# Edge stage of a four-layer graph network: TensorE in source order, layer 0's products spread over the batches, edge arrays loaded alone, and a short last batch

## The chip, the cores and the metric

The kernel runs on one core of a Trainium2 chip. The metric is the device time of one execution in microseconds. A core has TensorE (PE, with its weight loads shown apart as PEld), VectorE (DVE), ScalarE (ACT), GpSimd (POOL) and SyncE (SP). SP, ACT and POOL also issue DMA transfers, which 16 DMA engines carry out.

## What is computed

There are 3125 nodes with 128 features each, and 103,125 edges (`src`, `dst`, `edge_weight`) sorted by `dst`. Four layers follow one another, each with a residual and a layer norm:

```python
x = _layernorm(x + _L0_gnn_ref(x, src, dst, edge_weight, ...))  # relu(segment_sum(w * (x @ W)[dst], src) + b)
x = _layernorm(x + _L1_gnn_ref(x, edge_index, ...))             # four attention heads over the edges, skip, norm
x = _layernorm(x + _L2_gnn_ref(x, ...))                         # attention over the edges, one head
x = _layernorm(x + _L3_gnn_ref(x, edge_index, ...))             # two mean aggregations, sigmoid
```

The kernel turns the edges into two dense matrices over (dst, src), padded to 3200 x 3200: `wd` in DRAM, float32, holds the sums of the edge weights, and `f_ctd` in DRAM, bf16, holds the number of edges. Layer 0 multiplies with `wd`; the other layers use `f_ctd`.

## The kernel before, in words

`fast_path` does the work (`general_path` stands in a branch that runs only if a check at the end fails).

**Front.** The three edge arrays are loaded (lines 584 to 586; `dst` and the weights by SP, `src` by ACT), VectorE and ScalarE pack them into `tab` (628 to 630), and SP and ACT store it to the DRAM table `td` (633). POOL then gathers from `td` five groups of 128 windows (648, tile `eg`). A window is five destination rows; it gets 256 consecutive edges. In the program the load of `x` (642, 644) stands ahead of the gathers, and the 25 loads of weights, biases and attention vectors (through `load` at 540, and 713) are on ACT's DMA queue; some of them are issued before the edges' table is stored.

**Keys.** `keys_of(g)` (from line 655) turns group `g` into keys: VectorE and ScalarE make `kic`, `kid` and `wei` (661 to 669), TensorE transposes them in six pieces into PSUM (674 to 676), and copies out of PSUM give `kd2`, `kc2` and the three bf16 parts of the weight (534, 536, 689, 692, 693). Groups 0 and 1 are made in the front, groups 2 to 4 while batches 9, 17 and 25 run (`make(b)`, at `b % 8 == 2`).

**Edge stage.** There are NBT = 40 batches of BW = 16 windows, 640 windows, though 625 hold the 3125 rows. `make(b)` has VectorE write one-hot matrices for the batch's 32 half-windows: `ohd` and `ohc` (826), and `wod`, the first times each part of the weights (835); ScalarE makes a quarter of the last part (844). `make(b + 1)` stands ahead of batch b's products. A batch has four groups of four windows. For a group TensorE runs eight products into `cp` (866) and 24 into `wp` (874); ScalarE copies them out to `cs` (879) and `ws` (885). `cp` and `wp` share three PSUM banks. The tiles `ohd` and `ohc` have two buffers each, `wod` six (two batches), `ws` and `cs` two. After a batch SP stores `ws` to `wd` (887, two transfers, pieces of 512 bytes), and after every second batch `cs` to `f_ctd` (890, pieces of 320 bytes).

**Layer 0's products.** The sum over nodes runs over 25 blocks of 128 rows of `wd`. For the first Z0 = 20 column blocks `add0` (786) loads a block's rows in two tiles `cw` (792, 640 KB each; three buffers) and runs 20 products, 40 TensorE instructions, in one go (796). The loop calls it for a block once its rows are stored: `while acc0 and (done + 1) * P <= (b - 1) * BW * WN`. Blocks that are left after the loop follow it. The remaining five column blocks are added after the stage, in tiles `left` (PSUM) out of 320 KB loads. `xw_of` (747) makes `xw = x @ W` in batches 0 and 1, and `products_of_weights` (728 to 743) small products in batch 2.

**Order.** Each engine's order of instructions is set by a scheduler from the program; none of it is fixed by hand. DMA transfers of one queue are issued in that queue's order, and an issue can wait for an earlier transfer to land.

After the edge stage come layer 1 (from about 545 us of the profile), layer 2 and layer 3. The change doesn't touch them.

Of the kernel before, what the change touches and what calls it, by code (L numbers as in the profile page):

```python
# [7 lines left out]
F32 = mybir.dt.float32  # L8
# [486 lines left out]
NBT = NW // BW  # L495
Z0 = 20
# [11 lines left out]
def fast_path(  # L508
# [29 lines left out]
    def load(name, ap, shape):  # L538
        t = cst.tile(shape, F32, name=name)
        nc.scalar.dma_start(t, ap)  # L540
        return t
# [100 lines left out]
    nc.sync.dma_start(x[:, 0:NF, :], x_in[0 : NF * P, :].rearrange("(b p) d -> p b d", p=P))  # L642
    nc.gpsimd.memset(x[:, NF, :], 0.0)
    nc.sync.dma_start(x[0:NR, NF, :], x_in[NF * P : N, :])
    egs = []
    for g in range(NG):
        eg = ep.tile([P, EW // 16, 3, 16], F32, name="eg", bufs=3)
        nc.gpsimd.indirect_dma_start(
# [3 lines left out]
        egs.append(eg)  # L652

    def keys_of(g):

        eg = egs[g]
        kd2 = kp.tile([P, P // BW, 2, BW, 2], BF16, name="kd2")
        kc2 = kp.tile([P, P // BW, 2, BW, 2], BF16, name="kc2")
        w2 = [kp.tile([P, P // BW, 2, BW, 2], BF16, name=f"w2_{s}") for s in range(3)]
# [10 lines left out]
        t0 = cps.tile([P, 4, P], F32, name="t0", tag="cw")  # L670
        t1 = cps.tile([P, 2, P], F32, name="t1", tag="cw")
        for h in range(2):
            a = slice(h * P, (h + 1) * P)
            nc.tensor.transpose(t0[:, h, :], kid[:, a], ident)
            nc.tensor.transpose(t0[:, 2 + h, :], kic[:, a], ident)
            nc.tensor.transpose(t1[:, h, :], wei[:, a], ident)
# [9 lines left out]
        for h in range(2):  # L686
            copy(kd2[:, :, h, :, :], pairs(t0, h))
            copy(kc2[:, :, h, :, :], pairs(t0[:, 2:, :], h))
            nc.scalar.copy(w2[0][:, :, h, :, :], pairs(t1, h))
        for s, (i, o) in enumerate(((t1, wt), (wt, wu))):  # L690
            for h in range(2):
                nc.vector.tensor_tensor(each(o, h), each(i, h), w2[s][:, :, h, :, 0], OP.subtract)
                nc.scalar.copy(w2[s + 1][:, :, h, :, :], pairs(o, h))
        return kd2, kc2, w2, wu

    keys = {0: keys_of(0), 1: keys_of(1)}


    l0_wt = load("f_l0_wt", l0_w, [P, P])
# [11 lines left out]
    for s, a in enumerate((l1_as, l1_ad)):  # L711
        for h in range(H):
            nc.scalar.dma_start(att[h * C : (h + 1) * C, s * H + h : s * H + h + 1], a[h, :].rearrange("(c o) -> c o", o=1))
# [72 lines left out]
    def add0(pool, i, accs, blocks):  # L786

        b0, n = blocks
        for h in range(0, n, 10):
# [5 lines left out]
            for j in range(h, h + m):  # L795
                nc.tensor.matmul(  # L796
                    accs[j // 4][:, j % 4, :], cw[:, j - h, :], xw[:, i, :], start=False,
                    stop=(i == NB - 1 and (j % 4 == 3 or j == n - 1)), skip_group_check=True,
                )
# [12 lines left out]

    def make(b):

        if b % 8 == 2 and 8 < b < NBT - 8:
            keys[b // 8 + 1] = keys_of(b // 8 + 1)
# [7 lines left out]

        for o, k in ((ohd, kd2), (ohc, kc2)):
            nc.vector.tensor_tensor(  # L826
                o.rearrange("p w (a t) -> p w a t", t=2), twos(k),
                ramp.rearrange("p (a t) -> p a t", t=2)[:, None, :, :].to_broadcast([P, 2 * BW, P // 2, 2]),
                OP.is_equal,
            )  # L830
        wod = []
        for s in range(3):
            f = of_.tile([P, 2 * BW, P], BF16, name="wod")
            n = 2 * BW if s < 2 else BW
            nc.vector.tensor_tensor(  # L835
                f[:, 0:n].rearrange("p w (a t) -> p w a t", t=2), ohd[:, 0:n].rearrange("p w (a t) -> p w a t", t=2),
                twos(w2[s])[:, 0:n], OP.mult,
            )
            wod.append(f)

# [9 lines left out]
    done = 0  # L850
    cur = make(0)
    for k in range(0, BW, 4):
        cur[3](k)
    for b in range(NBT):
        ohd, ohc, wod, _ = cur
        cur = make(b + 1) if b + 1 < NBT else None
        if b % SB == 0:
# [768 lines left out]
```

## Time and profile before

| what | us |
|---|---|
| median of three runs | 1529.78 (1528.83 to 1531.31) |
| profiled execution | 1529.55 |
| its span, first to last instruction | 1527.5 |
| PE, DVE, ACT, POOL busy in the span | 1395.1, 978.3, 921.5, 127.8 |
| first gather of edges issued (POOL) | 23.28 |
| first one-hot matrix begun (DVE) | 31.67 |
| last one-hot work of the last batch ends (DVE) | 460.97 |
| last of layer 0's first 20 column blocks ends (PE) | 499.0 |

Times are microseconds from the span's start. A group's line gives the source line, the engine, the operation, the tiles written and read, the shapes, the count, then the busy time and the mean of one in ns, then the idle time of the engine before them with what ended it. A line of waits says which engine and line waited for which, and then the total, the number of waits and the longest. In the timeline each line is a start and a duration. In the table of stages each line is a stretch, its length, the busy time (and instructions) of PE, PEld, DVE, ACT and POOL, then the granted TensorE clock as a share of full speed, the share of the 16 DMA engines' time, and GB/s.

### The profile page before, as it was taken

To read this page: it belongs to the slowest core of one execution; us is meant where nothing else is said; L and a number is where in the kernel's file an instruction comes from. 1 tells how busy PE (TensorE), PEld (TensorE's weight loads), DVE (VectorE), ACT (ScalarE), POOL (GpSimd) and SP (SyncE) were. 2 spreads that over 40 slices of the span, in tenths; PEclk is the share of its full clock that TensorE was granted. 3 is DMA by queue.
4 is the path that set the end of the run, shared out by engine and by line. 5 is a ranking of instruction groups with operands and counts; after the bars stand their busy time and mean duration, and the time that the engine had idled before them with its cause. 6 is when DMAs were issued, how large, how long until landed. Compare 5 with 4: busy or idle time off the path is not lost. (4 is left out here: it accounts for less than half of the span.)

```text
span 1527.5 us, 35222 instructions
## 1 busy us (share of the span) xinstructions
PE 1395.1 (91%) x14871; PEld 1220.8 (80%) x14871; DVE 978.3 (64%) x1574; ACT 921.5 (60%) x1880; POOL 127.8 (8%) x162
## 2 busy tenths in 40 slices
PE   4899999999997987999989989899999989999995
PEld 3898999998997876889979979577777764458995
DVE  4999899999991389879978887444464360012005
ACT  2988778888882479878778677554465330023006
POOL 2000000000000023203212310300000000000000
PEclk9999999999999999999999999999999999999998
DMA  6387787887878633444434433232222227513551
GB/s 193 87 216 212 208 227 206 236 211 208 221 211 246 207 97 97 142 125 122 131 119 117 132 86 104 79 111 70 76 61 78 69 100 250 196 44 130 195 195 46
DMA packets 210370, 223.92 MB, mean 147 GB/s; under 512 B 72893, under 2 KB 184008, under 8 KB 209946
## 3 DMA queue, kind: packets, MB, share of 16 engines
q1 hardware_dynamic: 206344, 217.26, 48.9%
q10 hardware_dynamic: 3457, 2.35, 0.6%
q8 instruction: 118, 1.93, 0.5%
q0 software_dynamic: 400, 1.97, 0.4%
q14 instruction: 51, 0.41, 0.1%
HBM read 157.19 MB, written 64.36 MB: 145 GB/s over the span
## 5 line engine op out<-in xcount | busy, mean ns | idle before, releaser
L1243 PE MATMUL acc<-vp,cm 128*128 128x198 bf16 x2500 | 345.7, 253 | 7.5 <-DVE cm L1228 4.6
L1227 ACT ACTIVATE fm<-adr,bas 128x896 bf16<-128x896 f32 (+1 forms) x320 | 286.3, 952 | 67.6 <-DVE cm L1228 62.8
L1238 PE MATMUL acc<-vp,ct 128*128 128x204 bf16 x1250 | 315.3, 256 | 9.0 <-DVE vp L1146 4.5
L1243 PEld LDWEIGHTS <-cm 128*128 128x128 bf16 x2500 | 236.2, 98 | 26.8 <-issue 9.3
L874 PE MATMUL wp<-wod,ohc 128*128 128x128 bf16 x3840 | 244.0, 219 | 8.9 <-ACT cs L879 6.6
L874 PEld LDWEIGHTS <-ohc 128*128 128x128 bf16 x3840 | 224.0, 98 | 10.0 <-issue 9.5
L835 DVE TENSOR_TENSOR wod<-ohd,w 128x4096 bf16<-128x4096 bf16 (+1 forms) x120 | 225.0, 1929 | 0.6 <-PE wp L874 0.6
L1228 DVE TENSOR_TENSOR cm<-fm,ct 128x896 bf16<-128x896 bf16 (+1 forms) x320 | 196.6, 645 | 36.0 <-PE acc L1243 13.6
L844 ACT ACTIVATE wod<-ohd,wu 128x128 bf16<-128x128 bf16 x640 | 197.0, 399 | 0.0
L1382 DVE TENSOR_TENSOR e<-e,ct 128x416 f32<-128x416 f32 (+1 forms) x175 | 108.3, 625 | 106.2 <-ACT e L1381 98.1
L1381 ACT ACTIVATE e<-s,f_nm 128x416 f32<-128x416 f32 (+1 forms) x175 | 109.6, 633 | 97.8 <-PE s L1378 90.8
L1386 PEld LDWEIGHTS acc<-self__8127,e 128*128 128x128 f32 x1250 | 148.2, 193 | 20.6 <-issue 18.8
L1386 PE MATMUL acc<-self__8127,e 128*128 128x129 f32 x1250 | 148.6, 276 | 0.6 <-DVE e L1382 0.6
L1378 PE MATMUL s<-yT,f_xT 128*128 128x416 f32 (+1 forms) x350 | 142.8, 543 | 4.6 <-ACT rt L1358 4.0
L796 PE MATMUL acc<-f_xw,cw 128*128 128x128 f32 x1000 | 119.2, 279 | 7.5 <-DMA cw<-wd 7.5
L1238 PEld LDWEIGHTS <-ct 128*128 128x128 bf16 x1250 | 122.7, 98 | 2.6 <-issue 1.4
L885 ACT COPY ws<-wp 128x512 f32<-128x512 f32 x160 | 93.5, 585 | 49.9 <-PE wp L874 48.3
L796 PEld LDWEIGHTS acc<-f_xw,cw 128*128 128x128 f32 x1000 | 115.8, 195 | 7.8 <-DMA cw<-wd 7.7
L866 PE MATMUL cp<-ohc,ohd 128*128 128x125 bf16 x1280 | 96.7, 218 | 21.1 <-ACT ws L885 17.9
L1378 PEld LDWEIGHTS s<-yT,f_xT 128*128 128x128 f32 x350 | 62.1, 191 | 55.5 <-issue 39.2
L1555 PE MATMUL acc<-ip,ct 128*128 128x128 bf16 x1875 | 105.2, 219 | 0.0
L826 DVE TENSOR_TENSOR ohd<-kd,ramp 128x4096 bf16<-128x4096 bf16 x40 | 91.5, 2288 | 21.2 <-PE cp L866 21.1
(279 smaller groups left out, 1492.9 us busy)
## 6 DMA issues: line engine op xcount, KB each, us to landing
ct<-f_ctd SPq DMA_DIRECT2D x50, 800.0 KB
wd<-ws SPq DMA_DIRECT2D x40, 896.0 KB
ct<-f_ctd SPq DMA_DIRECT2D x150, 224.0 KB
cw<-wd SPq DMA_DIRECT2D x50, 640.0 KB
f_ctd<-cs SPq DMA_DIRECT2D x20, 1000.0 KB
ct<-f_ctd SPq DMA_DIRECT2D x25, 416.0 KB
ct<-f_ctd SPq DMA_DIRECT2D x25, 365.2 KB
cw<-wd SPq DMA_DIRECT2D x25, 320.0 KB
```

Of the source, the lines that this page charges most:

```text
L796: nc.tensor.matmul(accs[j // 4][:, j % 4, :], cw[:, j - h, :], xw[:, i, :], start=False, stop=(i == NB - 1 and (j % 4 == 3 or j == n - 1)) ...
L835: nc.vector.tensor_tensor(f[:, 0:n].rearrange("p w (a t) -> p w a t", t=2), ohd[:, 0:n].rearrange("p w (a t) -> p w a t", t=2), twos(w2[s] ...
L844: nc.scalar.activation(wod[2][:, BW + w, :], ohd[:, BW + w, :], AF.Copy, scale=w3[:, 1, at : at + 1])
L874: nc.tensor.matmul(wp[:, j, :], ohc[:, w, :], wod[s][:, w, :], start=(j == 0 and q == 0 and s == 0), stop=(j == 3 and q == 1 and s == 2), ...
L1227: nc.scalar.activation(f[:, : n * P], at, AF.Relu, bias=bas[:, c, h : h + 1], scale=UP)
L1228: nc.vector.tensor_tensor(m[:, : n * P], f[:, : n * P], ct[:, : n * P], OP.min)
L1238: nc.tensor.matmul(out_(F1, PW), ct[:, k * P : (k + 1) * P], vp[:, c, hp : hp + 2, :, 2 * F1 : V1], start=(c == 0), stop=False, skip_group ...
L1243: nc.tensor.matmul(out_(0, 2 * F1)[:, j], ms[j][:, k * P : (k + 1) * P], vp[:, c, hp + j, :, 0 : 2 * F1], start=False, stop=(c == NB - 1 a ...
L1378: nc.tensor.matmul(s[:, :m], xT[:, c * P : (c + 1) * P], yT[:, i0 * P + a : i0 * P + a + m], start=True, stop=True)
L1381: nc.scalar.activation(e[:, a : a + m], s[:, :m], AF.Exp, bias=nm[:, q : q + 1], scale=scale)
L1382: nc.vector.tensor_tensor(e[:, a : a + m], e[:, a : a + m], ct[:, a : a + m], OP.mult)
L1386: nc.tensor.matmul(acc[k // 3][:, (k % 3) * (P + 1) : (k % 3 + 1) * (P + 1)], es[q, c][:, k * P : (k + 1) * P], vo[:, c, 0 : P + 1], start ...
```

## The change

1. From batch 3 on, TensorE's instructions keep the program's order (`manual_schedule` for PE) until the end of the edge stage. The scheduler still orders the other engines.
2. `adds0` issues a block's loads at once and returns its 20 products as a list. The loop runs them from the next batch on: three after each group, four after the second, 13 a batch.
3. The load of `x` waits (through two POOL memsets of `x`) until the second gather is issued; the weights' loads go to SP's queue behind `x`, with the exception of `l0_wt` and `l0_br`.
4. `keys_of` is split: `columns_of` two batches ahead, at `b % 8 == 1`, and the transposes at `b % 8 == 3`. The transposes go through two PSUM tiles that ScalarE copies to SBUF (`k_` in bf16, `w_`), and the other copies read those. Group 1 is no longer made in the front.
5. The last batch has LW = 4 windows and one group in place of four; VectorE writes 4 windows per half there. 628 windows give 3140 rows; the remaining 60 rows of `wd` are filled with zeros by six stores after batch 6 (10 rows each, in pieces of 25 numbers, 100 bytes). The unused columns of the last `cs` are set to zero by POOL.
6. The last store of `f_ctd` is issued by ACT.

```diff
 def load(name, ap, shape):
     t = cst.tile(shape, F32, name=name)
-    nc.scalar.dma_start(t, ap)
+    with tc.issue_after(x_load.ins):
+        nc.sync.dma_start(t, ap)
     return t
...
-    nc.sync.dma_start(x[:, 0:NF, :], x_in[0 : NF * P, :].rearrange("(b p) d -> p b d", p=P))
-    nc.gpsimd.memset(x[:, NF, :], 0.0)
-    nc.sync.dma_start(x[0:NR, NF, :], x_in[NF * P : N, :])
     egs = []
     for g in range(NG):
...
+        if g == 1:
+            with tc.issue_after(got.ins):
+                nc.gpsimd.memset(x[:, 0:1, 0:1], 0.0)
+                nc.gpsimd.memset(x[:, NF, :], 0.0)
+    x_load = nc.sync.dma_start(x[:, 0:NF, :], x_in[0 : NF * P, :].rearrange("(b p) d -> p b d", p=P))
+    nc.sync.dma_start(x[0:NR, NF, :], x_in[NF * P : N, :])
...
+    def keys_of(kid, kic, wei):
...
+        k_ = ep.tile([P, 4, P], BF16, name="k_")
+        w_ = ep.tile([P, 2, P], F32, name="w_")
+        t = cps.tile([P, 4, P], F32, name="t", tag="cw")
         for h in range(2):
...
+            nc.tensor.transpose(t[:, h, :], kid[:, h * P : (h + 1) * P], ident)
+            nc.tensor.transpose(t[:, 2 + h, :], kic[:, h * P : (h + 1) * P], ident)
+        nc.scalar.copy(k_, t)
+        t = cps.tile([P, 4, P], F32, name="t", tag="cw")
+        for h in range(2):
+            nc.tensor.transpose(t[:, h, :], wei[:, h * P : (h + 1) * P], ident)
+        nc.scalar.copy(w_, t[:, 0:2, :])
...
-    keys = {0: keys_of(0), 1: keys_of(1)}
+    keys = {0: keys_of(*columns_of(0))}
...
-    def add0(pool, i, accs, blocks):
+    def adds0(pool, i, accs, blocks):
...
+        todo = []
...
-                nc.tensor.matmul(
+                todo.append(lambda j=j, a=cw[:, j - h, :]: nc.tensor.matmul(
...
+        return todo
...
-        if b % 8 == 2 and 8 < b < NBT - 8:
-            keys[b // 8 + 1] = keys_of(b // 8 + 1)
+        if b % 8 == 1 and b < NBT - 8:
+            keys[b // 8 + 1] = columns_of(b // 8 + 1, marked)
+        if b % 8 == 3 and b < NBT - 8:
+            keys[b // 8 + 1] = keys_of(*keys[b // 8 + 1])
...
+        def some(s):
+            if b < NBT - 1:
+                return [slice(0, 2 * BW if s < 2 else BW)]
+            return [slice(0, LW)] + ([slice(BW, BW + LW)] if s < 2 else [])
...
+        nw = BW if b < NBT - 1 else LW
+        todo += soon
+        soon.clear()
...
-        for k in range(0, BW, 4):
+        for k in range(0, nw, 4):
...
             nc.scalar.copy(ws[:, k : k + 4, :], wp)
+            m = 4 if k == 4 else 3
+            for f in todo[:m]:
+                f()
+            del todo[:m]
...
+        if b == 6:
+            nc.vector.memset(none, 0.0)
+            for i in range(NL * WN, NP, 10):
+                with tc.issue_after(stored.ins):
+                    nc.sync.dma_start(
+                        wd[i : i + 10, :].rearrange("i (p k) -> p i k", p=P), none.rearrange("p (i k) -> p i k", k=NB)
+                    )
...
+            eng = nc.scalar if b == NBT - 1 else nc.sync
+            eng.dma_start(ctd[:, :, i0 : i0 + SB * BW * WN].rearrange("c d i -> d c i"), cs)
...
+            order = ExitStack()
+            order.enter_context(tc.manual_schedule(engines={mybir.EngineType.PE}))
         while acc0 and (done + 1) * P <= (b - 1) * BW * WN:
-            add0(zp, done, acc0, (0, Z0))
+            soon += adds0(zp, done, acc0, (0, Z0))
             done += 1
+    for f in todo + soon:
+        f()
+    order.close()
     for i in range(done, NB):
         add0(zp, i, acc0, (0, Z0))
```

In the changed kernel's own order of SP's queue the six zero stores stand directly behind the stores of batch 6, and directly ahead of the loads of block 2 (rows 256 to 383).

## The prediction

> **What bounds the kernel now.** I read the page first. PE is busy in 91% of the span, but its chain of waits is mostly in later layers, which the change leaves alone. So I took the edge stage (31 to 499 us) apart: VectorE's groups and waits there, then the timelines of DVE, PE and the front.
>
> VectorE's groups and its longest wait between 30 and 500 us:
>
> ```profile
> L835 DVE TENSOR_TENSOR wod<-ohd,w 128x4096 bf16<-128x4096 bf16 (+1 forms) x120 | 225.0, 1929 | 0.6 <-PE wp L874 0.6
> L826 DVE TENSOR_TENSOR ohd<-kd,ramp 128x4096 bf16<-128x4096 bf16 x40 | 91.5, 2288 | 21.2 <-PE cp L866 21.1
> L826 DVE TENSOR_TENSOR ohc<-kc,ramp 128x4096 bf16<-128x4096 bf16 x40 | 91.4, 2284 | 0.0
> ...
> DVE ohd L826 <- PE cp L866: 21.1, 16, 1.7
> ```
>
> VectorE is the stage's pace: 225 + 91.5 + 91.4 = 408 us of a stretch of 429 (31.67 to 460.97). It stands still only where PE frees `ohd` late, 16 times, 21.7 us with the 0.6 above. The cause is PE's order:
>
> ```profile
> 425.11 0.60 PE L866 MATMUL cp<-ohc,ohd 128*128 128x125 bf16 x8
> 425.55 1.50 PE L874 MATMUL wp<-wod,ohc 128*128 128x128 bf16 x24
> 426.89 0.60 PE L866 MATMUL cp<-ohc,ohd 128*128 128x125 bf16 x8
> ...
> 428.28 4.68 PE L796 MATMUL acc<-f_xw,cw 128*128 128x128 f32 x40
> 432.80 0.55 PE L874 MATMUL wp<-wod,ohc 128*128 128x128 bf16 x7
> ```
>
> A group takes 426.89 - 425.11 = 1.78 us, a batch of four 7.12. A block of layer 0 holds PE for 432.80 - 428.28 = 4.52 us at once, 0.226 per product. A block is due every 128/80 = 1.6 batches, so PE needs 7.12 + 4.52/1.6 = 9.95 us a batch on the mean. VectorE's own batch (ohd 450.97 to the end of wod 460.97, less overlap) is 2.2 + 2.2 + 5.54 = 9.95 too. Both engines are level, and 4.5 us lumps make one wait for the other.
>
> The stage's end, PE's timeline, then two stretches of one microsecond (the clock and the DMA share are the last but two and last but one columns):
>
> ```profile
> 470.90 9.24 PE L796 MATMUL acc<-f_xw,cw 128*128 128x128 f32 x80
> 487.63 11.39 PE L796 MATMUL acc<-f_xw,cw 128*128 128x128 f32 x80 [7.49 <-DMA cw<-wd]
> ```
> ```profile
> 482.00:483.00 1.00, 0.00 (x0) 0.00 (x0) 0.00 (x0) 0.00 (x0) 0.00 (x0) 1.00 1.22 249
> ...
> 488.00:489.00 1.00, 1.00 (x6) 1.00 (x6) 0.00 (x0) 0.00 (x0) 0.00 (x0) 0.50 1.04 430
> ```
>
> Four blocks are left when the edges end; two of them wait 7.5 us for loads that queue behind the last `f_ctd` store, and the idle PE falls to half its clock (0.50) and needs until 492 to recover, some 2.4 us lost. From VectorE's end to the stage's end: 499.0 - 461.0 = 38.0 us.
>
> The front: the timeline has the table's store issued at 13.78 and the gather at 23.28.
>
> ```profile
> 13.78 1.69 SPq L633 DMA_DIRECT2D td<-tab  x1
> ...
> 23.28 1.20 POOL L648 DMA_INDIRECT eg<-td,row_i  x1 [11.86 <-DMA f_att<-in_L_gnn_att_dst_dram]
> ...
> 27.62 0.35 DVE L661 TENSOR_SCALAR kic<-eg,thr 128x256 f32<-128x256 f32 x1 [9.82 <-DMA eg<-td,row_i]
> ```
>
> **The change, part by part** (against the profiled execution: 1529.55, of which 2.05 lie outside the span; the median of the three runs, 1529.78, is the same).
>
> *Front, gain 5.5.* The last piece of `src` is issued at 5.26, behind weights; without them at about 3.7, and it took 2.6 to be read (7.96): about 1.6 earlier. Three casts leave VectorE's way to `tab`: 0.4. So `td` is stored at 11.8. Its 1.25 MB then share the engines with nothing; before, the 1.57 MB of `x` lay ahead. Bounds: 9.5 us as now, or 3.6 (1.25 MB at the 350 GB/s of that stretch) plus 1.5; I take 7.0, so the gather goes at 18.8 and `kic` follows 4.3 later (23.28 to 27.62), with half a us for the `x` beside it at 23.7, 3.9 earlier. From `kic` to the first one-hot is 4.05 now; the new path adds a copy (0.6, as `ws`) but makes `ohc` first: about 3.2. Only one group's keys are made: the last `wod` of batch 0 ends at 26.9 + 2.2 + 0.5 + 2.2 + 0.5 + 5.5 = 37.8, now 43.3. The later `x` (issued near 22, landed near 30) is needed at 31.8 at the earliest. Its 25 followers on SP lie ahead of the first `wd` store, at about 45; if the attention vectors' small loads hold SP as they hold ACT's queue now (6.2 + 2.7 us) they end near 36. Uncovered, that costs up to 5.
>
> *Spreading, gain 21.7.* A group with three products takes 1.78 + 0.68 = 2.46, a batch with 13 products 10.06; no lump is left. Fixed order asks that ACT keep up: two copies at 0.47 apart and four activations at 0.295, 2.1 us a group, under 2.46.
>
> *Keys, about 0, then a cost of 4.5.* VectorE pays 0.6 (kic, kid) plus about 1.5 for four groups (its `kc` copies read SBUF; 0.17 to 0.42 each by the small casts and the present `kc`, 0.25 taken), about as much as now. But ACT now runs six copies ahead of `cs` and waits for VectorE's `wt` and `wu`; `ws` of the second group then comes near 9.7 us after the batch's start while PE wants its bank at 8.3. About 1.5 us for each of three groups; bounds 0 and 4.6 in all by ACT's present waits there (`kd` on `kc`, 4.6).
>
> *Last batch, gain 7 on VectorE.* Nine operations on 4 windows at 0.28 (an eighth of 2.29) to 0.4, 3.0 in all, in place of 9.95. PE: one group, 1.78, in place of 7.12. A zeroing on idle POOL is hidden by 30 batches of slack.
>
> *The tail.* 22 blocks and part of the 23rd are run in the loop by the loop's arithmetic (13 a batch; 27 products are left at the end of batch 38). Batch 38 needs 10.06 after VectorE ends it. Then one group, 27 products (6.1), and blocks 23 and 24 (9.1); loads are bounded by three buffers and the last stores, so I count 20, not 17. ACT's own issue of the last `f_ctd` takes it out of SP's way.
>
> *Zero stores, the one new cost that I think shows: 13.* 60 rows go out as 60 x 128 = 7680 pieces of 100 bytes. They stand behind batch 6's store and ahead of block 2's loads on SP, and PE, in fixed order, reaches block 2 after two groups and seven older products of batch 7, plus a third group: 2.46 + 2.69 + 1.78 = 6.9 us on. The nearest row is `f_ctd`: pieces of 320 bytes moved at 203 to 259 GB/s in 480 to 485, 14.4 GB/s an engine, 22 ns a piece. Then 480 pieces an engine take 10.6 us, from about 3.5 us into the batch (after the 1.02 MB of `wd`), and the 640 KB load lands near 17.5: PE stands for 10.6 and pays 2.4 at half clock. No row has pieces under 320 bytes written in number: at half the price the stall is 5, at double 21 to 26; if PE lags or the loads slip past, 0. I take the row's own 22 ns.
>
> [...]
>
> [...]
>
> *Sum.* VectorE: 37.8, seven batches of 9.95 and two key items (2.1) give 109.5; batch 7 on PE takes 10.06 + 13: 132.6. From there PE is the later engine: 31 batches at 7.12 = 220.7, 387 products at 0.2266 = 87.7, transposes 2.0, plus 4.5 (keys), 3 (three loads issued within 8 us of their need, one every eight batches) and 2 (batches in which VectorE is longer): 452.5. Tail 20: 472.5 against 499.0, so 26.5 less: **1503**. The rest of the kernel should shift as a whole.
>
> **Rivals.**
> - *Zero stores hidden.* VectorE then runs on to 424.3 for batch 38; 10.1 + 3 + 20 give 459, about 40 less: 1489 (1486 to 1496). For: DMA engines are 0.79 to 0.84 busy there, not full. Against: one queue, in order, and a PE that can't pass the load.
> - *Zero stores at double price, or more loads late:* gains of 5 to 19, 1510 to 1526.
> - *Slower: loads late for every block.* PE cannot run another group while a `cw` is missing. The DMA share rises with the faster batch, 0.82 x 10.75/10.1 = 0.87. If each of 22 blocks makes PE wait, each us of it costs 22 us; from 1.4 us a block on, the 29.5 to the slower side is eaten, and at 2 us it would be about 1547. Against: a load now takes some 9 us from issue to use even behind 2 MB of stores, and most are issued 10 us or more ahead.
> - *No effect:* the front and the last batch alone give 5.5 + 7, so this needs a new wait of the same size.
>
> **Chances.** Forecast (1496 to 1510) 0.45; hidden 0.22; dearer but faster 0.20; within 0.2%, about what a measurement of this kernel can tell from no change, 0.03; slower 0.10. Faster 0.87. The range 1485 to 1522 takes in the first two cases and most of the third.
>
> **What would show it.** `kic` near 23.7 and the first full `wod` at 37.8; VectorE's waits for `cp` gone outside batch 7 to 9; one PE wait for `cw` of some 10 us near 116, with a clock of 0.5 after it; the stage ending near 472. Wrong: repeated PE waits for `cw`, or for `ws` in ordinary batches, or a wait of PE at `x` or SP at the weights in the front.

## The result and the profile after

| | before | after |
|---|---|---|
| median of 4 runs each, taken in turn (us) | 1529.43 (1528.83 to 1531.31) | 1542.78 (1540.93 to 1545.23) |
| ratio, 95% interval | | 1.0085 (1.0072 to 1.0098) |
| span of the profiled execution (us) | 1527.5 | 1539.7 |
| mean granted TensorE clock | 0.981 | 0.966 |
| edge stage ends (us) | 499.0 | 511.4 |

The change is slower by 13 us; 1503 was forecast, and even the range's upper end, 1522, is missed. The whole loss lies in the edge stage: it ends 12.4 us later, the span 12.2.

VectorE's groups of the changed kernel from 20 to 545 us, and its longest wait there (sum, times, longest):

```profile
L881 DVE TENSOR_TENSOR wod<-ohd,w 128x4096 bf16<-128x4096 bf16 (+2 forms) x122 | 221.4, 1865 | 0.4 <-PE wp L926 0.4
L870 DVE TENSOR_TENSOR ohd<-kd,ramp 128x4096 bf16<-128x4096 bf16 (+1 forms) x41 | 90.1, 2199 | 46.8 <-PE cp L918 46.8
L870 DVE TENSOR_TENSOR ohc<-kc,ramp 128x4096 bf16<-128x4096 bf16 (+1 forms) x41 | 89.8, 2192 | 0.4 <-PE wp L926 0.2
...
DVE ohd L870 <- PE cp L918: 46.8, 28, 20.0
```

VectorE's work went down by 6.6 us (401.3 for 407.9), nearly the 7 of the last batch. Its wait for PE, which the change was to remove, went up from 21.1 to 46.8 us, and one wait of 20.0 is nearly half of it. PE's timeline in batch 7 of the changed kernel shows what PE did then:

```profile
118.70 1.11 PE L821 MATMUL acc<-f_xw,cw 128*128 128x128 f32 x8
119.65 0.60 PE L918 MATMUL cp<-ohc,ohd 128*128 128x125 bf16 x8
120.09 1.50 PE L926 MATMUL wp<-wod,ohc 128*128 128x128 bf16 x24
141.72 1.65 PE L821 MATMUL acc<-f_xw,cw 128*128 128x128 f32 x6 [20.13 <-DMA cw<-wd]
143.16 1.05 PE L918 MATMUL cp<-ohc,ohd 128*128 128x125 bf16 x8
144.00 1.85 PE L926 MATMUL wp<-wod,ohc 128*128 128x128 bf16 x24
```

PE stands for 20.13 us in front of one product of block 2, whose `cw` isn't there; the groups behind it have all they need. SyncE's queue in the same time (start, time taken by the issues), and the stretches of 5 us (after the engines' busy times: granted clock, DMA share, GB/s):

```profile
106.06 11.74 SPq L943 DMA_DIRECT2D wd<-ws  x4
117.85 12.39 SPq L948 DMA_DIRECT2D wd<-none  x6
130.35 4.57 SPq L817 DMA_DIRECT2D cw<-wd  x3
```
```profile
120.00:125.00 5.00, 1.59 (x29) 1.42 (x26) 4.29 (x6) 4.73 (x15) 0.00 (x0) 0.92 1.21 102
125.00:130.00 5.00, 0.00 (x0) 0.00 (x0) 0.00 (x0) 0.00 (x0) 0.00 (x0) 0.50 1.53 42
130.00:135.00 5.00, 0.00 (x0) 0.00 (x0) 0.00 (x0) 0.00 (x0) 0.00 (x0) 0.50 1.28 38
135.00:140.00 5.00, 0.00 (x0) 0.00 (x0) 0.00 (x0) 0.00 (x0) 0.00 (x0) 0.50 0.95 117
```

The six zero stores (`wd<-none`) stand ahead of the loads, their issue alone takes SyncE 12.39 us, and while they run the transfer engines are full (share over 1) but move only 38 to 42 GB/s. At 40 GB/s over 16 engines a piece of 100 bytes takes 40 ns; the forecast took 22. All four engines stand still, and PE's clock falls to 0.50.

The same shape comes back in small every eighth batch. PE's timeline in batch 15, then stretches of 1 us:

```profile
224.61 1.50 PE L926 MATMUL wp<-wod,ohc 128*128 128x128 bf16 x24
228.90 0.94 PE L821 MATMUL acc<-f_xw,cw 128*128 128x128 f32 x6 [2.79 <-DMA cw<-wd]
229.67 0.70 PE L918 MATMUL cp<-ohc,ohd 128*128 128x125 bf16 x8
230.17 2.77 PE L926 MATMUL wp<-wod,ohc 128*128 128x128 bf16 x24
```
```profile
228.00:229.00 1.00, 0.10 (x1) 0.10 (x1) 0.08 (x2) 0.77 (x3) 0.00 (x0) 1.00 1.01 415
...
230.00:231.00 1.00, 1.00 (x14) 1.00 (x11) 0.52 (x1) 0.58 (x1) 0.00 (x0) 0.52 0.71 292
231.00:232.00 1.00, 1.00 (x13) 1.00 (x11) 1.00 (x1) 0.00 (x0) 0.00 (x0) 0.50 0.15 55
```

A wait of 2.79 us is followed by some 3 us at half the clock, in which 24 matmuls take 2.77 us instead of 1.50. The length of the wait doesn't decide this. A longer one, in batch 23, leaves the clock at 1.00, and a shorter one, in batch 36, halves it (the last section says when):

```profile
317.07 0.94 PE L821 MATMUL acc<-f_xw,cw 128*128 128x128 f32 x6 [3.57 <-DMA cw<-wd]
...
318.28 1.50 PE L926 MATMUL wp<-wod,ohc 128*128 128x128 bf16 x24
...
461.77 0.49 PE L821 MATMUL acc<-f_xw,cw 128*128 128x128 f32 x2 [2.36 <-DMA cw<-wd]
...
462.87 2.77 PE L926 MATMUL wp<-wod,ohc 128*128 128x128 bf16 x24
```

The front and the end of the stage, from the timelines of all engines, of PE and of SyncE:

```profile
10.53 0.54 SPq L635 DMA_DIRECT2D td<-tab  x1
...
19.64 1.20 POOL L647 DMA_INDIRECT eg<-td,row_i  x1 [17.18 <-DMA td<-tab]
...
23.51 0.35 DVE L671 TENSOR_SCALAR kic<-eg,thr 128x256 f32<-128x256 f32 x1 [7.28 <-DMA eg<-td,row_i]
...
33.30 0.66 PE L773 MATMUL trx<-f_ident,f_x 128*128 128x128 f32 x2 [7.64 <-DMA f_x<-in_x_dram]
```
```profile
485.03 4.01 PE L821 MATMUL acc<-f_xw,cw 128*128 128x128 f32 x34
...
497.24 14.21 PE L821 MATMUL acc<-f_xw,cw 128*128 128x128 f32 x100 [7.09 <-DMA cw<-wd]
```
```profile
473.82 11.47 SPq L943 DMA_DIRECT2D wd<-ws  x4
485.39 1.78 SPq L817 DMA_DIRECT2D cw<-wd  x1
487.26 3.94 SPq L943 DMA_DIRECT2D wd<-ws  x2
491.31 20.98 SPq L817 DMA_DIRECT2D cw<-wd  x6
```

`kic` is 4.1 us earlier than before (27.62). But `x` now lands at 33.3, where PE had its first transposes of it at 19.56. At the end 50 products wait 7.09 us, because block 22's second load is issued only at 485.39, behind the stores of batches 37 and 38, which SyncE had to wait for.

The most useful view is worked out from VectorE's timeline: the time from one batch's `ohd` instruction to the next. It is 9.95 us where VectorE is the pace. Number n is from `ohd` of batch n to that of batch n+1; since `ohd` has two buffers, a late batch of PE shows one number later (PE's batch 7 in number 8). Experiments are included, and all values are in us:

| n | before | after | E1 | E4 | E5 | E9 | E15 |
|---|---|---|---|---|---|---|---|
| 2 | 9.95 | 11.10 | 12.60 | 11.59 | 11.95 | 12.42 | 9.94 |
| 3 | 9.94 | 14.01 | 14.01 | 14.00 | 14.02 | 14.00 | 12.70 |
| 4 | 9.95 | 11.05 | 11.05 | 11.05 | 11.05 | 11.05 | 10.05 |
| 8 | 9.94 | 30.52 | 16.95 | 13.76 | 10.42 | 10.42 | 10.42 |
| 10 | 11.63 | 10.24 | 10.24 | 10.24 | 11.97 | 25.16 | 11.59 |
| 11 | 11.68 | 11.95 | 11.96 | 11.96 | 11.95 | 11.96 | 11.96 |
| 13 | 9.94 | 10.24 | 10.24 | 10.24 | 10.24 | 10.24 | 10.24 |
| 16 | 10.91 | 12.91 | 13.77 | 14.27 | 10.42 | 10.42 | 10.42 |
| 24 | 10.91 | 13.58 | 13.36 | 13.71 | 10.42 | 10.42 | 10.42 |
| 32 | 10.91 | 13.80 | 13.83 | 13.09 | 9.95 | 9.94 | 9.94 |
| 38 | 9.94 | 14.27 | 14.70 | 14.34 | 10.02 | 10.02 | 10.01 |
| `ohd` of batch 8 at | 113.84 | 113.80 | 115.23 | 114.25 | 114.57 | 115.2 | 113.13 |
| from there to batch 39 | 337.1 | 358.1 | 346.4 | 342.1 | 327.0 | 341.2 | 325.8 |

So against before: nothing gained up to batch 8, 21.0 us lost in batches 8 to 38, and 8.6 gained from the last batch's `ohd` to the stage's end (39.5 us for 48.0). The sum is the 12.4.

### The profile page after: what moved, and what is told of

Its sections match the earlier page's. It is cut to its first block, busy times and chain, and to the rows that moved or that the text cites. A ratio compares the mean times of both kernels' runs of the same rounds, so it can differ in the third digit from the quotient of the medians.

```text
span 1539.7 us, 35023 instructions
## 1 busy us (share of the span) xinstructions
PE 1394.9 (91%) x14762; PEld 1224.3 (80%) x14775; DVE 971.7 (63%) x1579; ACT 921.0 (60%) x1872; POOL 132.5 (9%) x164
## 5 line engine op out<-in xcount | busy, mean ns | idle before, releaser
L881 DVE TENSOR_TENSOR wod<-ohd,w 128x4096 bf16<-128x4096 bf16 (+2 forms) x122 | 221.4, 1865 | 0.4 <-PE wp L926 0.4
L821 PE MATMUL acc<-f_xw,cw 128*128 128x128 f32 x1000 | 145.7, 288 | 39.3 <-DMA cw<-wd 39.3
L821 PEld LDWEIGHTS acc<-f_xw,cw 128*128 128x128 f32 x1000 | 126.4, 197 | 40.4 <-DMA cw<-wd 40.3
L931 ACT CAST cs<-cp 128x500 bf16<-128x500 f32 x157 | 90.4, 576 | 53.2 <-PE cp L918 51.7
L870 DVE TENSOR_TENSOR ohd<-kd,ramp 128x4096 bf16<-128x4096 bf16 (+1 forms) x41 | 90.1, 2199 | 46.8 <-PE cp L918 46.8
L937 ACT COPY ws<-wp 128x512 f32<-128x512 f32 x157 | 90.6, 577 | 29.3 <-PE wp L926 28.2
L1448 PEld LDWEIGHTS s<-yT,f_xT 128*128 128x128 f32 x350 | 62.2, 191 | 55.4 <-issue 39.4
```

Source lines behind the costliest of these rows:

```text
L821: todo.append(lambda j=j, a=cw[:, j - h, :]: nc.tensor.matmul(accs[j // 4][:, j % 4, :], a, xw[:, i, :], start=False, stop=(i == NB - 1 an ...
L881: made = nc.vector.tensor_tensor(packed(f, ww), packed(ohd, ww), twos(w2[s])[:, ww], OP.mult)
L1448: nc.tensor.matmul(s[:, :m], xT[:, c * P : (c + 1) * P], yT[:, i0 * P + a : i0 * P + a + m], start=True, stop=True)
```

## The experiments

The theory formed from this: PE takes its instructions in one fixed order, so a load that comes late for one product stops everything, and the change puts its loads behind stores. **A** is the part of it with the zero stores, **B** the loads of every eighth batch. The main rival (**R1**): PE has no time to spare anyway (13 products and four groups take it 10.24 us against VectorE's 9.95), so the waits only show where it runs out. Each ratio is against the kernel before, run on the same chip in turn; DVE waits are those of `ohd` for `cp`, and PE waits those for `cw`, both from 100 to 450 us. The last column is the end of the edge stage in the profiled execution. The layers behind it, which no edit touches, take 1026.1 to 1032.8 us in these profiles (1028.5 before), so a few microseconds between two rows can come from there.

| | kernel | us | ratio (95% interval) | DVE waits | PE waits | stage ends |
|---|---|---|---|---|---|---|
| | before | | 1 | 21.1 | 0 | 499.0 |
| | after | 1542.8 | 1.0085 (1.0072 to 1.0098) | 37.5 | 29.8 | 511.4 |
| E1 | zero stores in large pieces | 1531.5 | 1.0002 (0.9989 to 1.0015) | 25.3 | 17.1 | 501.0 |
| E2 | zero stores spread | 1543.0 | 1.0078 (1.0062 to 1.0095) | 34.8 | 26.5 | 511.8 |
| E3 | PE's order free | 1547.8 | 1.0112 (1.0096 to 1.0129) | 26.1 | 13.5 | 514.9 |
| E4 | padding kept | 1531.8 | 1.0002 (0.9991 to 1.0012) | 21.7 | 15.7 | 499.9 |
| E5 | E1 + early loads | 1515.5 | 0.9908 (0.9886 to 0.9930) | 11.8 | 7.3 | 481.2 |
| E6 | E5 + blocks a batch sooner | 1518.0 | 0.9928 (0.9904 to 0.9952) | 17.0 | 7.6 | 487.4 |
| E7 | E6 + 13 products in a burst | 1522.0 | 0.9949 (0.9932 to 0.9966) | 24.1 | 0 | 493.8 |
| E8 | E1 + front's loads undone | 1528.2 | 0.9983 (0.9973 to 0.9993) | 26.6 | 18.6 | 498.9 |
| E9 | after + early loads | 1532.2 | 1.0007 (0.9997 to 1.0017) | 26.0 | 19.1 | 495.4 |
| E10 | E4 + early loads | 1518.3 | 0.9914 (0.9897 to 0.9930) | 13.3 | 6.6 | 488.7 |
| E11 | E5 + front's loads undone | 1514.2 | 0.9897 (0.9878 to 0.9917) | 12.6 | 7.9 | 481.3 |
| E12 | E11 + last `f_ctd` behind | 1510.8 | 0.9861 (0.9841 to 0.9880) | 12.7 | 7.8 | 478.5 |
| E13 | E12 + PE's order free | 1529.1 | 0.9990 (0.9977 to 1.0002) | 27.7 | 0 | 495.0 |
| E14 | before + front's loads alone | 1538.1 | 1.0051 (1.0034 to 1.0068) | | | 503.8 |
| E15 | E12 + half loads | 1505.9 | 0.9843 (0.9827 to 0.9860) | 10.6 | 3.8 | 472.7 |

### What the zero stores cost: E1, E2, E4

**E1.** The same 10 rows per store, written as one run instead of row by row:

```diff
-wd[i : i + 10, :].rearrange("i (p k) -> p i k", p=P), none.rearrange("p (i k) -> p i k", k=NB)
+wd[i : i + 10, :].rearrange("i d -> (i d)").rearrange("(p k) -> p k", p=P), none
```

> The changed kernel with the same six zero stores in pieces of 1000 B (each 10 rows of the table written as one run of 32,000 floats, 250 a partition) where the change has 100 B: 768 pieces for 7,680. Theory A (the price of the small pieces, and TensorE's fixed order behind them): the wait of 20.1 us for cw at 141.7 falls below 2 us, the clock of 0.50 at 126 to 144 goes, and the time is 1542.8 - 20 = 1523 (1519 to 1527). Rival R1 (TensorE is short of time anyway: the products at 0.24 us in threes and a clock that is taken back): the gain of the stall is lost in later batches and the time stays over 1532. Rival R2 (the stall hangs on the place of the six DMAs, ahead of block 2's loads, and not on their pieces): the wait stays over 10 us and the time over 1535.

Measured: 1531.5, 11.3 less. From SyncE's and PE's timelines of this kernel, and the two stretches in which the large pieces pass:

```profile
119.14 5.20 SPq L948 DMA_DIRECT2D wd<-none  x6
```
```profile
129.58 1.65 PE L821 MATMUL acc<-f_xw,cw 128*128 128x128 f32 x6 [6.69 <-DMA cw<-wd]
```
```profile
122.00:124.00 2.00, 0.90 (x17) 0.72 (x13) 2.00 (x1) 2.00 (x7) 0.00 (x0) 1.00 0.72 210
124.00:126.00 2.00, 0.00 (x0) 0.00 (x0) 1.73 (x5) 2.00 (x7) 0.00 (x0) 1.00 0.86 200
```

The engines move 200 to 210 GB/s in all where the small pieces gave 40, and number 8 of the table falls by 13.6. The pieces are the price, as theory A has it, and R2 falls (the edit changes the pieces' size and their places in a row together; no run separates the two). But A's time and its wait "below 2 us" are missed: 6.69 us of wait stay, and numbers 16, 24, 32 and 38 are as long as they were. R1's bound of 1532 is all but reached, so this run doesn't decide about R1. The loss had more than one cause.

**E2.** One zero store of 100-byte pieces behind each of batches 6 to 11:

```diff
-if b == 6:
-    for i in range(NL * WN, NP, 10): ...
+if 6 <= b < 12:
+    i = NL * WN + 10 * (b - 6)   # one store
```

> The changed kernel with the six zero stores in their 100 B pieces, but one behind each of the batches 6 to 11. Theory A: each takes 16.5/6 = 2.8 us of the 16 transfer engines and moves the loads behind it by that; loads that land less than 2.8 us before their products are late, the others hide it; total wait for cw in batches 7 to 12 between 2 and 9 us where it was 20.1, time 1524 to 1533. Rival R1: over 1535, since TensorE loses the time elsewhere. Rival R2 (place alone decides): the first of the six, still ahead of block 2's loads, keeps over 10 us of the wait.

Measured: 1543.0, no gain. The wait at block 2 falls to 6.47, below R2's 10, but one of 13.20 appears at 197: the scheduler put four loads behind the sixth zero store. The 1280 pieces of one store take 2.2 to 3.3 us to pass, where the changed kernel's six stores take 17.8 in all. This run therefore tells that small pieces don't get cheap by being dealt out. What they cost in the end it doesn't tell, since the loads were moved too, and so it doesn't decide about R1 either.

**E4.** `LW = 16`, no zero stores, all else as changed:

```diff
-LW = 4
+LW = 16
```

> The changed kernel with a full last batch of 16 groups, as before, and so without the six zero stores; front, keys, spreading and fixed order as in the change. Theory A: the 22 us of stall and half clock go, the last batch costs TensorE 5.3 and VectorE 7 us again; 1542.8 - 22 + 6 = 1527 (1522 to 1532), so the edit 'no padding groups' is worth +16 as built. Rival R1: over 1535. Rival R4 (the short last batch is worth more than the zero stores cost): 1543 or more.

Measured: 1531.8, in A's range: as built, leaving the padding out costs 11 us. With no zero store at all, block 2 still waits 3.17 us, and numbers 8, 16, 24, 32 and 38 are 13.1 to 14.3. These are theory B's.

### What the loads' place costs: E5, E6, E9

By the loop's arithmetic, PE uses 13 products a batch, and in batches 7, 15, 23 and 31 only 7 products stand ahead of a block that was taken up at the end of the batch before. They cover 6.9 us. Its loads are issued behind that batch's stores, which wait for ScalarE's last copy: in batch 15 of the changed kernel at 223.34, 4.4 us after the batch began, for a product due at 226.1. (In batches 14, 22, 30 and 38 the loop leaves no older product ahead at all, and PE doesn't wait. For two of them the trace shows why: the scheduler put the loads ahead of the stores, block 6's at 202.09 and batch 13's stores at 210.21, block 21's at 462.11 and batch 37's at 473.82.) Number 38 is another case of a late place: the second load of block 20 is issued at 455.69, behind batch 35's `f_ctd` and stores, for a product that PE reaches at 459.4 in batch 36.

**E5.** The take-up is moved ahead of the batch's stores:

```diff
+while acc0 and (done + 1) * P <= (b - 1) * BW * WN:
+    soon += adds0(zp, done, acc0, (0, Z0)); done += 1
 for a, e in ((0, 112), (112, KW)):
     stored = nc.sync.dma_start(wv_[b * BW : ...], ws[a:e, 0:nw, :])
...
-while acc0 and (done + 1) * P <= (b - 1) * BW * WN: ...
```

> The zero stores in large pieces, and the loads of cw issued ahead of a batch's own stores on SyncE instead of behind them (same blocks in the same batch, same three buffers). The times between VectorE's ohd instructions with large pieces show 3.5 to 4.5 us over the rest at every eighth batch (16.95, 13.77, 13.36, 13.83 where the others are 10.24 or less) and 14.70 before the last. Theory B (in those batches the list of products has run dry, so the first product wants a load that was only issued behind the stores of the batch before): these five fall to about 10.3, PE's waits for cw between 80 and 480 us from 20 to below 5, and the time is 1531.5 - 17 = 1514 (1510 to 1520). Rival R1 (TensorE's own work is the bound and waits only move): over 1526. Rival R6 (the loads wait for a free buffer, not for their place): the waits stay, over 1526.

Measured: 1515.5 where B said 1514. The five long numbers fall to 10.0 to 10.4. SyncE's timeline, PE's largest wait before the stage's end, and VectorE's wait from 100 to 450 us:

```profile
113.52 1.23 SPq L817 DMA_DIRECT2D cw<-wd  x2
116.86 1.84 SPq L946 DMA_DIRECT2D wd<-ws  x2
118.74 7.38 SPq L951 DMA_DIRECT2D wd<-none  x6
```
```profile
140.41 0.71 PE L821 MATMUL acc<-f_xw,cw 128*128 128x128 f32 x4 [2.28 <-DMA cw<-wd]
```
```profile
DVE ohd L870 <- PE cp L918: 11.8, 16, 2.0
```

Block 2's loads now go at 113.52, ahead of batch 6's own stores and the zero stores. This falsifies R1: PE's work is the same, and the time is not. It also rules out R6 for these five numbers, since the buffers are the same. The stage ends 19.8 us earlier than in E1; the layers behind it took 4 us longer in this profile. The wait of 2.28 is new and belongs to another block (number 10 of the table).

**E6.** Each block is taken up one batch sooner still:

```diff
-while acc0 and (done + 1) * P <= (b - 1) * BW * WN:
+while acc0 and (done + 1) * P <= b * BW * WN:
```

> As the kernel with early loads, and each block is taken up one batch sooner (as soon as its stores have been issued in the batch before), so blocks 22 and 23 are loaded before the last batch's stores and 20 products instead of 50 stand behind TensorE's last wait. Theory B: besides the five late loads, 30 products at the half clock (some 8 us) leave the tail; 1504 to 1512. Rival R6 (three buffers: an earlier take-up only waits for a buffer and holds the stores up behind it on SyncE): not faster than with early loads, 1514 or more.

Measured: 1518.0, not faster than E5, and the stage ends 6.1 us later. As in E5, 40 products stand behind the last wait and not the 20 expected, and numbers 11, 22 and 30 rise to 14.00, 14.16 and 12.15. This agrees with rival R6: with three buffers an earlier take-up waits for a buffer, at the head of SyncE's queue.

**E9.** The changed kernel with E5's edit alone, its zero stores in 100-byte pieces:

> The changed kernel with the one edit that the loads of cw are issued ahead of a batch's own stores; the zero stores keep their 100 B pieces and now stand behind block 2's loads. Theory A (some 16 us of the transfer engines whatever stands behind them, and only loads that are near their products pay): the loads of block 3 and the stores of batch 7 are behind them, two batches ahead of need; 2 to 8 us of wait near 130 to 145 and a time of 1517 to 1523, against 1515.5 with large pieces. Rival R8 (their price is additive, 13.6 us as between small and large pieces with late loads): 1529.

Measured: 1532.2, 16.7 above E5. R8 (additive) is nearer than A. From SyncE's and PE's timelines:

```profile
119.34 14.01 SPq L951 DMA_DIRECT2D wd<-none  x6
133.46 8.73 SPq L946 DMA_DIRECT2D wd<-ws  x2
142.24 1.05 SPq L957 DMA_DIRECT2D f_ctd<-cs  x1
143.38 4.64 SPq L817 DMA_DIRECT2D cw<-wd  x2
```
```profile
152.00 1.23 PE L821 MATMUL acc<-f_xw,cw 128*128 128x128 f32 x4 [13.33 <-DMA cw<-wd]
```

The stall has only moved to the next loads: they go at 143.38, behind the zero stores, batch 7's stores and an `f_ctd`. Two batches of distance in the program were no distance on the queue.

### What the fixed order and the spreading are worth: E3, E7, E13

**E3.** The changed kernel without `manual_schedule`; groups and products are emitted as before, the scheduler places them:

```diff
-order.enter_context(tc.manual_schedule(engines={mybir.EngineType.PE}))
```

> The changed kernel with the fixed TensorE order taken off: products and groups are emitted in the same spread order, and the scheduler places them by its own estimates, as in the kernel before. Theory A (in a fixed order each late load stops the groups too): the stall of 20.1 us shrinks, since groups can stand ahead of products, but the scheduler puts products in bursts again, so part of VectorE's 21 us of waits comes back; 1525 to 1538. Rival R3 (the order is no part of it, a late load would stop the scheduler's order as well): 1540 or more.

Measured: 1547.8, 5.0 above the fixed order, so R3's number, and in part R3's reason. One late load still stops PE for 13.5 us in the scheduler's order, and VectorE with it (14.3 us at `wod`, which the table's column doesn't count). ScalarE's copies hold PE up as well (11.9 us for `cp` alone, 2.4 in the fixed order), and bursts are back. So the fixed order isn't what made the change slow; the late loads stop either order. **E13** puts the same question to the kernel whose loads are early:

> The kernel with early loads, front undone, large zero stores and the last f_ctd store behind the loads, with the fixed TensorE order taken off. Theory G (spreading in a fixed order is worth what VectorE then no longer waits: it waits 14.2 us for ohd in all with the order fixed, 21.1 in the kernel before with bursts of 20): 4 to 10 us above the fixed order's 1510.8, 1515 to 1521. Rival R3 (with early loads the order is without effect): within 2.5 of 1510.8. Rival R5 (as predicted, the spreading itself is worth 21.7): 1528 or more.

Measured: 1529.1 against E12's 1510.8, 18.3 more: beyond theory G, in the region of R5. VectorE's waits from 100 to 450 us, first with the order free, then E12's with it fixed:

```profile
DVE ohd L867 <- PE cp L915: 27.7, 14, 4.4
```
```profile
DVE ohd L867 <- PE cp L915: 12.7, 16, 2.6
```

So spreading in a fixed order is worth about what the prediction gave it, if the loads are there. The bursts aren't the whole of it: with the order free PE waits 20.7 us for ScalarE's copies, with the order fixed 2.4.

**E7.** E6 with up to 13 products behind a batch's last group, in the fixed order:

```diff
-m = 4 if k == 4 else 3
+m = 13 if k == nw - 4 else 0
```

> As the kernel whose blocks are taken up a batch sooner, but up to 13 products stand together behind a batch's last group, in TensorE's fixed order, instead of 3, 4, 3 and 3 behind its four groups. Theory C (the even 13 a batch and the loads' lead matter, where in the batch they stand does not, and consecutive products take 0.2266 us each for 0.24): a batch of TensorE takes 7.12 + 2.95 = 10.07 for 10.24; within 4 us of the spread kernel, likelier below. Rival R5 (as predicted: spreading inside a batch is what takes VectorE's waits away): VectorE waits again some 0.7 us a batch, 20 us and more in all, and the time is 15 us or more above the spread kernel.

Measured: 1522.0, 4.0 above E6 (the intervals overlap; the stage ends 6.5 us later), at the edge of theory C. VectorE's waits come as R5 has them (24.1 us for 17.0), but not the 15 us that R5 puts on them. By subtraction, some 4 to 6 of the 18 us come from dealing the products out to the four groups and the rest from holding PE to an even 13 a batch. That is argued from kernels whose loads differ, not shown.

### What the front is worth: E8, E11, E14

**E8** (on E1) and **E11** (on E5) issue `x` and the weights as the kernel before did; the deferred second group of keys stays:

```diff
+x_load = nc.sync.dma_start(x[:, 0:NF, :], ...)   # ahead of the gathers
-    with tc.issue_after(x_load.ins):
-        nc.sync.dma_start(t, ap)
+    nc.scalar.dma_start(t, ap)
```

> The changed kernel with zero stores in large pieces, and with the loads of x and of the weights issued as in the kernel before (x ahead of the table's store on SyncE, the weights on ScalarE's queue). Theory D (the front's 5.5 us are given back in batches 1 to 3, where TensorE has to do the work on x that it did before in the time before the first batch): kic near 27.6 again, but VectorE's ohd of batch 8 still between 113 and 117 us, and the time within 3 of 1531.5. Rival R7 (the front counts in full, as predicted): 1536 or more.

> Early loads, zero stores in large pieces, and the loads of x and the weights issued as in the kernel before. Theory D (TensorE's work on x belongs ahead of batch 0; undoing the front gained 3.4 us with late loads): 1515.5 - 3 = 1512 (1510 to 1514). Rival R7 (the gain there came from other late loads being moved about): 1515 or more.

Measured: 1528.2 (3.3 below E1, the intervals overlap by a little) and 1514.2 (1.3 below E5, intervals overlapping, between the figures of the two theories; the stage ends at the same time). R7 of E8, a loss of 5 us, falls: the front's loads as changed gain nothing. That undoing them gains anything isn't shown. **E14** is the kernel before with those loads alone moved:

> The kernel before with one part of the change alone: x loaded behind the second gather and the weights behind x, all on SyncE; keys of both first groups are still made ahead. Theory D (kic earlier by some 3.5 us, but TensorE's work on x moves into batches 0 to 3 and takes it back): ohd of batch 8 at 113 to 116 us where it is 113.8, and the time within 3 of before, 1528 to 1534. Rival R7 (the front counts, as predicted): 1526.5 or less.

Measured: 1538.1, 8 us slower, worse than theory D allowed. `kic` is at 23.53, yet PE's first work on `x` is late:

```profile
32.94 1.09 PE L755 MATMUL trx<-f_ident,f_x 128*128 128x128 f32 x4 [3.19 <-DMA f_x<-in_x_dram]
```

By batch 1 it is 2.5 us ahead of before (40.80 for 43.28), by batch 8 2.7 behind (116.58 for 113.84): PE's transposes and products of `x`, done before at 19 to 37 us while it had nothing else, now stand between the groups of batches 0 to 3. That gives back the 2.5 and costs 2.7 of the 8 (8.7 in the profiles). Another 2.1 arise in the rest of the stage, where the scheduler's order differs, and 3.9 behind the stage; their cause stays open.

### The short last batch and the tail: E10, E12, E15

**E10** is E4 with E5's early loads: a full last batch and no zero stores.

> The kernel with early loads, a full last batch of 16 groups and so no zero stores. Theory E (the stage ends with the last loads of cw behind the last stores, and VectorE's shorter last batch only makes TensorE wait for them): 1514 to 1519, within 3 of 1515.5. Rival R9 (as predicted, the short batch is worth 7 us on VectorE's path): 1520.5 to 1524.

Measured: 1518.3 against 1515.5, in theory E's range, intervals almost the same. In the profiles, however, the stage ends 7.5 us later, and 4.2 of these lie behind the last batch's `ohd` (43.9 us for 39.7). So a part of what the short batch saves VectorE, up to 4 us, does reach the end of the stage there; the time of the whole kernel doesn't show it clear of noise. E10 also lacks the zero stores, so it isn't the short batch alone that differs.

**E12** puts the last `f_ctd` store behind the last loads of `cw`:

```diff
-eng = nc.scalar if b == NBT - 1 else nc.sync
-eng.dma_start(ctd[:, :, i0 : ...], cs)
+if b < NBT - 1:
+    nc.sync.dma_start(ctd[:, :, i0 : ...], cs)
...
 add0(zp, i, acc0, (0, Z0))
+with tc.issue_after(loads[-1].ins):
+    nc.sync.dma_start(ctd[:, :, i0 : ...], cs)
```

> As the kernel with early loads and the front undone, and the last store of f_ctd (1000 KB) on SyncE behind the last loads of cw instead of on ScalarE's queue ahead of them. Theory F (that store shares the transfer engines with the last stores and loads; 1000 KB at the 250 GB/s of that stretch is 4 us): TensorE's last wait of 6.2 us falls to about 2, 2 to 4 us below the kernel without this edit, 1508 to 1510. Rival R10 (the wait is the latency of store, then load, and not their rate): no change, within 1.

Measured: 1510.8, 3.3 below E11 (the intervals just touch), the size of theory F. PE's last wait, in E11 and then in E12:

```profile
470.65 10.62 PE L815 MATMUL acc<-f_xw,cw 128*128 128x128 f32 x80 [6.61 <-DMA cw<-wd]
```
```profile
467.87 10.66 PE L817 MATMUL acc<-f_xw,cw 128*128 128x128 f32 x80 [4.79 <-DMA cw<-wd]
```

It falls by 1.8 and not to 2. What is left fits R10's way from the last store to the load, or a wait for a buffer; E15 tests the buffers.

**E15** gives `cw` six buffers of 5 blocks for three of 10:

```diff
-for h in range(0, n, 10): ...   # tile [P, 10, P], bufs=3
+for h in range(0, n, 5): ...    # tile [P, 5, P], bufs=6
```

> The kernel with early loads, front undone, large zero stores and the last f_ctd store behind, with cw in six buffers of 5 blocks (320 KB a load) for three of 10. Theory R6 (the waits left near 141, 226, 310 and 395, 2.9, 2.0, 1.4 and 1.6 us, and the 4.8 at the end, are loads that wait for a buffer): three of the four go and the end falls by 1 to 2, 4 to 8 us below 1510.8. Theory B (place and not buffers): the waits stay, within 2 of 1510.8; more loads on SyncE could cost 1 to 2.

Measured: 1505.9, 4.9 below E12, in R6's range, though the intervals overlap. PE's waits for `cw` from 100 to 450 us halve (7.8 to 3.8), but three are left where R6 had one. The end:

```profile
462.89 3.62 PE L817 MATMUL acc<-f_xw,cw 128*128 128x128 f32 x30 [3.50 <-DMA cw<-wd]
466.83 5.85 PE L817 MATMUL acc<-f_xw,cw 128*128 128x128 f32 x50 [0.33 <-DMA cw<-wd]
```

The stage ends at 472.7, 5.8 us before E12's, in the fastest of the four executions. This version beats both kernels: 0.9843 (0.9827 to 0.9860) of before.

## Why the prediction was wrong, point by point

The forecast put the end of the stage at 472.5; it came at 511.4, 38.9 later. E15 reaches 472.7, with other loads, buffers and front; that the two figures agree is chance, but it shows that the level was within reach once the loads came in time. Along the changed kernel's timeline the miss builds up so: batch 7 begins on PE at 114.4 for 109.5 (4.9, all of it lost in batches 2 to 4), batch 8 at 146.4 for 132.6 (8.9 more, the zero stores and the place of block 2's load), batch 38 ends at 483.3 for 452.5 (17.0 more, late loads and dearer products), and the stage at 511.4 for 472.5 (8.1 more, the tail). The steps:

- **Three loads issued late, "3 in all": the step that failed.** It saw the right places ("one every eight batches") and gave 1 us to each. The runs give 16.0 us for the loads' place (E5 against E1; 19.8 by the end of the stage). In the three batches that were meant (numbers 16, 24 and 32) it is 10.2 us where 3 were put, and numbers 8 and 38 add 6.5 and 4.7. Two things were left out. A load stands behind stores that themselves wait for ScalarE's copies, so it goes 4.4 us into the batch; and two of these three waits, with the one before number 38, were followed by some 3 us at half the clock. The tail's block 22 is late by the same place, but moving it ahead didn't shorten the tail (39.7 us behind the last `ohd` in E5, 39.4 in E1).
- **Zero stores, 13: mis-sized.** The mechanism was as written (in-order queue, in-order PE, stall at block 2, half clock), the price 40 ns a piece and not the 22 of the 320-byte row. The stall was 20.13 us for 10.6. Number 8 is 30.52, and 13.76 with no zero stores at all (E4), 16.8 us for the forecast's 13. The rival at double price put the stall at 21 to 26 and the time at 1510 to 1526: close for the stall, not for the time, since the rest was wrong too. What makes a piece of 100 bytes 1.8 times as dear as one of 320, no run shows.
- **Front, 5.5: right to batch 1, given back by batch 4.** `kic` at 23.51 (23.7 forecast) and `ohd` of batch 1 at 37.85 for 43.28 before, 5.4 us earlier. The working asked when PE needs `x` "at the earliest", not what PE had done with it while idle. It named a wait of PE at `x` as a sign of being wrong, and it came (7.64 us to 33.30). At batch 8 of VectorE nothing is left of the gain. It isn't all due to `x`: from batch 1 to 8 VectorE needs 76.0 us, before 70.6, and 72.5 in E8 and E11, which load `x` early but keep the second group's keys in batch 3. So some 1.9 go with those keys and the order there, for which the forecast had 2.1, and 3.5 with the late `x`.
- **Spreading, 21.7: near in size, conditional.** 18.3 between E13 and E12, in a kernel with early loads, and VectorE still waits 12.7 us there. In the change as built the waits it was to remove came back as others (46.8).
- **Products, 0.2266: mis-sized.** Three in a row between groups take 0.72, 0.24 each; a batch with 13 takes 10.24, not 10.06 (number 13). Over the stage that is some 5 us.
- **Keys, 4.5 and 2.0 for the transposes: somewhat high.** Numbers 11, 19 and 27 are 11.95, 1.7 over 10.24 each, 5.1 in all for 6.5. The wait for `ws` is there as written, but 0.8 us each, 2.4 in all.
- **Last batch, 7 on VectorE: done, but worth less.** Its operations took 3.6 us (3.0 forecast). By E10's profile at most some 4 us reach the end of the stage, and the time shows no difference clear of noise. The stores it needs made it cost 11 (E4).
- **Tail, 20: it took 28.2** from the end of batch 38 on PE (483.25) to 511.4: a wait of 7.09 and 50 products partly at half clock. E12 and E15 point at what it hung on: the store sharing the engines, and the buffers, some 3 and 5 us.
- **The rival "slower: loads late for every block"** had the right mechanism. It was given 0.10 because "most are issued 10 us or more ahead"; it did not need every block. The large wait at block 2, four of 2.4 to 3.6 us and the tail's 7.1 did it.
- **One slip in the working** changes little: 424.3 + 10.1 + 3 + 20 is 457.4 and not 459.

## What to carry to other kernels

A transfer that came late stopped PE here whether its order was written by hand (20.13 us in the changed kernel) or by the scheduler (13.5 us in E3): for each one, read where it stands on its queue and what the store ahead of it waits for, not how far apart the two stand in the program (in batch 15 the load went 4.4 us into the batch, behind stores that waited for ScalarE's last copy). The store in small pieces was priced by its pieces, 40 ns for each of 100 bytes, and it held up the loads behind it on that queue, early as they were written (13.33 us of wait in E9). And before moving an input later to speed up a chain, look at what the idle engines were doing with it: in E14 PE's work on `x`, done before in idle time at 19 to 37 us, came to stand between the groups of batches 0 to 3, and `ohd` of batch 8 went from 113.84 to 116.58 us.

## What the runs showed of the hardware

- Pieces of 100 bytes written in number moved at 38 to 42 GB/s with the engines full, 40 ns a piece and engine (changed kernel, 125 to 135 us); while the 1000-byte pieces of the same data passed, the engines moved 200 to 210 GB/s (E1, 122 to 126 us). Six stores of 1280 small pieces each also took SyncE 12.4 to 14.0 us to issue, for 5.2 to 7.4 with 128 pieces each. The number of pieces alone doesn't set that: E2's fourth store, of 1280 pieces, was issued in 0.41 us. In the kernel before, pieces of 512 bytes moved at 349 GB/s at 478 us and at 245 at 110 us, those of 320 bytes at 203 to 259 from 480 to 485 us: between these two sizes no clear price shows.
- PE's clock changed on a fixed grid. In each of the 17 profiles all changes of the granted clock lie whole multiples of 3.41 us apart (in the changed kernel at 124.23, 144.71, 230.04, 233.46, 404.12 and 407.54 us, for instance). What counted was how much of one such stretch PE was idle, and so where a wait fell, not how long it was. The 3.57 us up to 317.07 lie across two stretches, 55% idle and 50%, and the clock stays at 1.00; the 2.36 us up to 461.77 make one stretch 69% idle, and the clock falls at 462.15, when PE is at work again. Of the stretches between 42 and 480 us that began at full clock, all 35 that were idle for 57% or more were followed by half clock, and 2 of the 2074 others (idle time by the profile, in which the ends of matmuls are modelled). In the kernels before and after, these are all 4 stretches that were idle for 66% or more, and none of the 242 others, the idlest of which stood at 55%. So a stretch didn't have to be idle as a whole; one that was, in the kernel before from 482.01 us, was followed by half clock too, at 485.42.
- FP32 products of 128 x 128 cost 0.226 us in a run of 20 and 0.24 in runs of three between bf16 groups.
